# A second Strassen level for two of the seven products of the MLP gates, with the weight pass issued by GpSimd

## The chip, the cores and the metric

The kernel runs on one core of one Trainium2 chip. The metric is device time in microseconds (us), the median of several executions. One profiled execution stands beside it; all rows below come from that one.

## What is computed

A decoder layer on x of shape (2, 512, 1024), all in fp32. Only the parts around the change matter here:

```python
h  = res + mamba2(rmsnorm(res, ln1_w), ...)          # ends in y @ w_out.T
h2 = rmsnorm(h, ln2_w)
x  = x + h + silu(h2 @ gate_w.T) * (h2 @ up_w.T) @ down_w.T      # the MLP, inner width 3584
x  = x + cross_attention(layernorm(x), ctx)          # quantised to 8-bit codes
def _binary_diff_weight(w, base):
    d = w - base
    return base + mean(abs(d)) * sign(d)
x  = x + ffn(layernorm(x), W1, W3, W2)               # same form as the MLP, W_j = _binary_diff_weight(w_j, mean_w_j)
```

The three FFN weights need a mean over all of |w - base| before the first of them can be used. The kernel therefore makes one pass over w1, w3 and w2 (the weight pass) while the MLP runs.

## The kernel before, in words

**Stages.** In order of time: mamba up to its gated output; the out product (y @ w_out.T, 28 tiles on TensorE, L565) with the second RMS norm and its transposes (`finish`, L576 to L584), here called the turn; the MLP gates (about 470 to 1159 us); the MLP down product (to about 1490 us), with the cross-attention woven in; the FFN gates; the FFN down product.

**Tiling of the gates.** 3584 inner columns are cut into 14 groups of 256. A group has a gate weight and an up weight of 1024 x 256, and each is multiplied with the activations of 2 x 512 tokens as a 2x2 block product by Strassen's scheme in Winograd's form: seven block products instead of eight, each of them 4 matmuls of 128x128 by 128x512. Gate and up together take 56 such matmuls per group. The class `BlockProduct` (L227 to L272) holds one such product; `gates` (L649 on) runs the groups. `weight_blocks` makes the sums of weight blocks on VectorE (DVE), `act_blocks` (once) those of the activations. The seven products are added up on DVE from four PSUM banks. ScalarE (ACT) applies silu, DVE multiplies gate by up (L687), `hidden_blocks` and `down_blocks` (both through the helper at L192 and L195) make the sums of blocks that the down product needs, and these are stored in DRAM.

**The FFN gates** use another function, `gates2` (L766 on). There gate and up are stacked and a second level of Winograd's scheme is put on some of the seven products: products 1 and 2 (together) and 6 and 7 (together) become seven smaller products of four 128x256 matmuls each (`second_level`, L721 to L747), and the others (c: products 5 and 3, d: product 4) stay as 128x512 matmuls at L813.

**The weight pass.** `abs_sums` (L1008 on) is called once per MLP group. For each of the three weights it loads w and base on SyncE's queue (SP), 1 MB each (L177), subtracts on GpSimd (POOL, L1015), takes the sign into a bf16 tile on ACT (L1017), stores it from SP (L1018, 512 KB), and takes the absolute sum on ACT (L1019). All loads and stores of the MLP stand in one SP queue, in program order, and a waiting instruction holds up those behind it. For the first eight groups, ctx is turned to codes here too.

**What sets the order.** Each engine works through its own instructions in order. A scheduler lays out the streams from the order of the program; `tc.issue_after(x)` puts a piece no earlier than instruction x. In the FFN stage `in_turn` writes the order of TensorE (PE) out by hand. Pools give the number of buffers: one place for a gate weight and one for an up weight of the next group in `gates` (pool w, 2 places in all).

Of the kernel before, what the change touches and what calls it, by code (L numbers as in the profile page):

```python
# [37 lines left out]
def decoder(ctx, tc, a, out):  # L38
# [136 lines left out]
    def load_w(wp, tag, src, name, shape=(P, KC, GW)):  # L175
        wt = wp.tile(list(shape), F32, tag=tag, name=name)
        nc.sync.dma_start(wt, src)  # L177
        return wt
# [105 lines left out]
    def hidden_blocks(h):  # L284

        a11, a12, a22, a21, s2, s3, s4 = (h[:, i, :] for i in range(7))
        sub(s3, a11, a21)
        add(a21, a21, a22)
        sub(s2, a21, a11)
        sub(s4, a12, s2)  # L290

# [3 lines left out]
    with ExitStack() as m:  # L295
# [232 lines left out]
        scanned(1)  # L528

# [29 lines left out]

        def out_product(p, use):  # L560
            for t in range(TPB):
                ps = bank(count[0] % 4, f"op{p}_{t}")
                count[0] += 1
                for k in range(4):
                    nc.tensor.matmul(  # L565
                        ps, A[p][:, k, t * P : t * P + P], B[p][:, k, :], start=(k == 0), stop=(k == 3)
                    )
                use(t, ps)
# [4 lines left out]

        def finish(t):
            b = t // TPB
            if t % TPB == 0:  # L576
                h2T.append(actp.tile([P, KC, L], F32, tag="act", name=f"h2T{b}"))
            h2 = rows.tile([P, D], F32, tag="ra", name=f"h2_{t}")
            rr = rms_scale(f"rms2_{t}", xr[t], h2)
            nc.scalar.activation(h2, xr[t], AF.Identity, scale=rr)  # L580
            to_feature_major("h2T", trans, h2, h2T[b], t, ln2, split=False)
            x = rows.tile([P, D], F32, tag="ra", name=f"xa{t}")
            nc.sync.dma_start(x, a["x"][t * P : (t + 1) * P, :])
            nc.gpsimd.tensor_tensor(xr[t], xr[t], x, ALU.add)  # L584
# [37 lines left out]
        out_product(3, use3)  # L622
        out_product(4, use4)
        scan.close()

    POOLS = dict(t8=1, w=2, w1=2, raw=2, ap=1, sp=2, hp=1, tmp=7, p1=2, o12=2, o67=1, px=2, s23=1, s4=2, y12=1, y67=1, b4=2, t4=1)

    def open_pools(g, name, names):  # L630

        pl = {x: g.enter_context(tiles_waited(name=f"{name}{x}", bufs=POOLS[x])) for x in names}
        return pl

    def first_products(name, act, pl, gw, uw):

        first = {1: act[0][:, :4, :], 2: act[0][:, 4:, :]}
        both = []
        for odd, (x, w) in enumerate((("g", gw), ("u", uw))):
            p = BlockProduct((odd, 2 + odd, 4 + odd, 6 + odd), pl, f"{name}{x}0", {1: w[:, :4, :P], 2: w[:, 4:, :P]}, first)  # L640
            p.weight = w
            both.append(p)
        for p in both:
            p.begin()
        for p in both:
            p.c11()
        return both

    def gates(name, act, acts, g, pl, weights, side, begun):  # L649


        dram = [
            [tc.dram_tile([P, 7, 512], F32, name=f"{name}{x}d{i}") for i in range(NG)] for x in ("h", "w")
        ]
        with g:
            B = act_blocks(name, act, [pl["ap"].tile([P, 4, L], F32, tag=f"t{i}", name=f"{name}t{i}") for i in (2, 3, 4)])
            for i in range(NG):
                gw, uw, t8 = weights(i)
                if i in begun:
                    gate, up = begun[i]  # L660
                    for p in (gate, up):
                        p.A, p.B = weight_blocks(pl["sp"], p.name, p.weight), B
                else:
                    gate, up = (
                        BlockProduct(
                            (odd, 2 + odd, 4 + odd, 6 + odd), pl, f"{name}{x}{i}",
                            weight_blocks(pl["sp"], f"{name}{x}{i}", w), B,
                        )
                        for odd, (x, w) in enumerate((("g", gw), ("u", uw)))
                    )  # L670
                gc = gate.others() if i in begun else gate.whole()
                last = i == NG - 1

                def down_weights(t8, after):
                    with tc.issue_after(after):
                        down_blocks(t8[:, :4, :], t8[:, 4:, :])
                    nc.sync.dma_start(dram[1][i], t8[:, 1:, :])

                down_weights(t8, gate.last)
                sg = [gate.t("s")] + list(gc[1:])  # L680
                for o, c in zip(sg, gc):
                    nc.scalar.activation(o, c, AF.Silu)
                side(i, pl["raw"])
                uc = up.others() if i in begun else up.whole()
                h = pl["hp"].tile([P, 7, L], F32, tag="h", name=f"{name}h{i}")
                for slot, s_, u_ in zip((0, 3, 1, 2), sg, uc):
                    nc.vector.tensor_tensor(h[:, slot, :], s_, u_, ALU.mult)  # L687
                if last:
                    nc.sync.dma_start(dram[0][i][:, :3, :], h[:, :3, :])
                hidden_blocks(h)  # L690
                if last:
                    nc.sync.dma_start(dram[0][i][:, 3:, :], h[:, 3:, :])
                else:
                    nc.sync.dma_start(dram[0][i], h)
        acts.close()
        return dram
# [52 lines left out]
    def first_two(name, act, pl, i, gw, uw, banks):  # L749

        O = pl["o12"].tile([P, 2, 2, L], F32, tag="o", name=f"{name}o12_{i}")
        ps = []

        def step(p, x, w):
            if not p:
                ps.append(bank(banks[x], f"{name}a{x}_{i}"))
            for k in range(4):
                nc.tensor.matmul(  # L758
                    ps[x], w[:, 4 * p + k, :P], act[0][:, 4 * p + k, :],
                    start=not p and k == 0, stop=k == 3, skip_group_check=p > 0,  # L760
                )
            nc.scalar.copy(O[:, p, x, :], ps[x])  # L762

        return O, [lambda p=p, x=x, w=w: step(p, x, w) for p in range(2) for x, w in enumerate((gw, uw))]

    def gates2(name, act, acts, g, pl, weights, down_weight, begun, places):  # L766
# [4 lines left out]
        with g:  # L771
# [3 lines left out]
            ex = [x.rearrange("p a (b c d) -> p a b c d", b=2, c=2) for x in places]  # L775
            B67 = second_level_right(t23, ex[0][:, 0], ex[0][:, 1], ex[1][:, 0])
# [26 lines left out]
            for i in range(NG):  # L803
# [15 lines left out]
                if i in begun:  # L819
                    O12 = begun[i]  # L820
                else:
# [21 lines left out]
                if not last:  # L843
                    with tc.issue_after(turn):
                        if i + 1 not in begun:
                            A12 = outer_left(i + 1, *coming[0])
                        A, A67 = left(i + 1, *coming[0])
                if i == 0:
                    b = act[0].rearrange("p (q k) l -> p q k l", q=2)
                    B12 = second_level_right(b, ex[1][:, 1], ex[2][:, 0], ex[2][:, 1])  # L850
                if i + 2 < NG:
                    coming.append(weights(i + 2, stored))
                if not last:
                    w2.append(down_weight(i + 1, stored))
                t = pl["t4"].tile([P, 4, 512], F32, tag="t", name=f"{name}w{i}t")
                b = w2.pop(0)
                with tc.issue_after(turn):
                    down_blocks(b, t)
                nc.sync.dma_start(dram[1][i][:, :3, :], b[:, 1:, :])
                nc.sync.dma_start(dram[1][i][:, 3:, :], t)  # L860
# [132 lines left out]

    g = ExitStack()
    pl = open_pools(g, "m", ("t8", "w", "raw", "ap", "sp", "hp", "tmp", "p1"))
    cx = g.enter_context(tiles_waited(name="cx", bufs=1))
    sgp = g.enter_context(tiles_waited(name="sgp", bufs=2))

    def mlp_weights(i):
        gw = load_w(pl["w"], "w", a["gate_w"][i], f"gate{i}")  # L1000
        uw = load_w(pl["w"], "w", a["up_w"][i], f"up{i}")
        t8 = pl["t8"].tile([P, 8, 512], F32, tag="t8", name=f"down{i}")
        nc.sync.dma_start(t8[:, :4, :], a["down_w"][i])
        return gw, uw, t8
# [3 lines left out]
    def abs_sums(i, wp):  # L1008

        for j, (n, base) in enumerate(FFN):  # L1010
            w, b = (
                flat(load_w(wp, tag, a[x][i], f"s{x}{i}", (P, 4, 512) if n == "w2" else (P, KC, GW)))
                for tag, x in (("raw", n), ("base", base))
            )
            nc.gpsimd.tensor_tensor(w, w, b, ALU.subtract)  # L1015
            sg = sgp.tile([P, KC * GW], BF16, tag="sign", name=f"sg{n}{i}")
            nc.scalar.activation(sg, w, AF.Sign)  # L1017
            nc.sync.dma_start(signs[j][i], sg)  # L1018
            nc.scalar.activation(w, w, AF.Abs, accum_out=sums[:, j, i : i + 1])  # L1019
        if i < KC:  # L1020
            ctx_codes(i // 4, i % 4)

    loaded = [mlp_weights(0)]
    begun = first_products("m", h2T, pl, *loaded[0][:2])
    dram = gates("m", h2T, acts, g, pl, lambda i: loaded.pop() if loaded else mlp_weights(i), abs_sums, {0: begun})


# [276 lines left out]
```

## Time and profile before

| what | us |
|---|---|
| median of 3 executions (2448.77 to 2453.83) | 2449.19 |
| the profiled execution's own time | 2447.95 |
| its span, first to last instruction | 2446.1 |
| TensorE busy in the span | 2394.3 |
| granted TensorE clock, mean | 0.996 |
| the turn, 430 to 474 | 44.0 |
| MLP gates until the first down product (L911) | 474.0 to 1158.9 |
| most of the FFN gates | 1585 to 2143 |

How to read it: times are of one core. An engine's row gives busy time, number and mean duration of its instructions, and after the last bar its idle time ahead of them with what ended it ("<-"). fp32 matmuls appear as two records each, so a 128x512 matmul is two records of 0.429 us. PEclk is the share of full speed at which the chip let TensorE run. "DMA share" is the mean busy share of 16 DMA engines. In the timeline, a number in brackets is the idle time ahead of an instruction.

### The profile page before, as it was taken

To read this page: it belongs to the slowest core of one execution; us is meant where nothing else is said; L and a number is where in the kernel's file an instruction comes from. 1 tells how busy PE (TensorE), PEld (TensorE's weight loads), DVE (VectorE), ACT (ScalarE), POOL (GpSimd) and SP (SyncE) were. 2 spreads that over 40 slices of the span, in tenths; PEclk is the share of its full clock that TensorE was granted. 3 is DMA by queue.
4 is the path that set the end of the run, shared out by engine and by line. 5 is a ranking of instruction groups with operands and counts; after the bars stand their busy time and mean duration, and the time that the engine had idled before them with its cause. 6 is when DMAs were issued, how large, how long until landed. Compare 5 with 4: busy or idle time off the path is not lost.

```text
span 2446.1 us, 21791 instructions
## 1 busy us (share of the span) xinstructions
PE 2394.3 (98%) x8108; PEld 1485.6 (61%) x8116; DVE 1462.6 (60%) x2175; ACT 584.0 (24%) x704; POOL 314.6 (13%) x166
## 2 busy tenths in 40 slices
PE   7999999799999999999999999999999999999999
PEld 5445444444444444444888775567667667688888
DVE  4656676544544565444555656686675776665554
ACT  3222142443333433230000234332132221100000
POOL 1002020533323323220000010000000000000000
PEclk9999999999999999999999999999999999999999
DMA  3010032687888878875865480577667577686652
GB/s 139 35 52 18 18 121 100 236 325 297 345 313 336 342 314 339 312 297 180 250 186 166 123 264 35 154 202 198 190 181 203 166 197 207 221 259 193 201 168 65
DMA packets 177802, 486.00 MB, mean 199 GB/s; under 512 B 20768, under 2 KB 125216, under 8 KB 145696
## 3 DMA queue, kind: packets, MB, share of 16 engines
q1 hardware_dynamic: 171072, 436.37, 49.7%
q0 software_dynamic: 6624, 48.24, 9.6%
q8 instruction: 64, 1.05, 0.2%
q14 instruction: 42, 0.34, 0.0%
HBM read 345.07 MB, written 137.36 MB: 197 GB/s over the span
## 4 chain that ended last, share of the span: by engine, by line
PE 80%; DMA 7%; DVE 4%; POOL 4%; ACT 2%; issue 2%; SPq 1%; POOLq 0%; DVEq 0%; ACTq 0%
DMA smean_w<-in_mean_w 5%; POOL sw L1015 3%; PE op L565 3%; ACT sgw L1017 1%; DMA up<-in_up_w 1%; PE xa L1113 1%; DVE down L195 1%; PE dps L349 1%; PE fa L758 1%; PE y L485 1%; PE f0c L813 1%; PE f11c L813 1%; PE f10c L813 1%; PE f7c L813 1%; PE f4c L813 1%
## 5 line engine op out<-in xcount | busy, mean ns | idle before, releaser
L1015 POOL TENSOR_TENSOR sw<-sw,smean_w 128x2048 f32<-128x2048 f32 x42 | 196.6, 4681 | 405.5 <-DMA smean_w<-in_mean_w 401.3
L1017 ACT ACTIVATE sgw<-sw 128x2048 bf16<-128x2048 f32 x42 | 80.2, 1909 | 335.9 <-POOL sw L1015 335.9
L1195 POOL DMA_DIRECT2D fw<-in_mean_w x42 | 36.2, 861 | 527.6 <-ACT fw L1194 475.0
L1194 ACT ACTIVATE fw<-fsign,coeff 128x2048 f32<-128x2048 bf16 x38 | 76.1, 2004 | 93.6 <-DMA fsign<-sign 20.7
L1019 ACT ACTIVATE sw<-sw 128x2048 f32<-128x2048 f32 x42 | 80.2, 1909 | 0.9
L195 DVE TENSOR_TENSOR down<-down 128x512 f32<-128x512 f32 x56 | 77.7, 1408 | 0.7
L865 ACT ACTIVATE fo<-fo 128x512 f32<-128x512 f32 x56 | 35.0, 627 | 118.0 <-DVE fo L192 117.9
L511 POOL TENSOR_TENSOR mz<-mz,ys 128x512 f32<-128x512 f32 x16 | 20.7, 1293 | 309.2 <-DVE ys L508 277.1
L565 PE MATMUL op<-wout,mz 128*128 128x512 f32 x128 | 56.6, 592 | 0.0
L565 PEld LDWEIGHTS op<-wout,mz 128*128 128x128 f32 x128 | 23.9, 190 | 27.7 <-issue 27.5
L91 POOL TENSOR_TENSOR q_r<-q_e,mhalf 128x1 f32<-128x1 f32 x8 | 6.5, 806 | 260.9 <-DVE q_e L87 260.3
L867 DVE TENSOR_TENSOR fh<-fo 128x512 f32<-128x512 f32 x56 | 36.1, 682 | 1.5
L758 PE MATMUL fa<-x3T,fw 128*128 128x512 f32 x64 | 30.1, 624 | 2.1 <-ACT fo L762 2.1
L118 PE MATMUL h1T<-ident,h 128*128 128x128 f32 x64 | 15.2, 384 | 16.3 <-ACT h L340 10.4
L195 DVE TENSOR_TENSOR fh<-fh 128x512 f32<-128x512 f32 x42 | 29.0, 689 | 1.0
L195 DVE TENSOR_TENSOR mh<-mh 128x512 f32<-128x512 f32 x42 | 28.8, 686 | 0.5
L192 DVE TENSOR_TENSOR hid<-hid,op 128x512 f32<-128x512 f32 x24 | 15.9, 683 | 21.3 <-PE op L565 21.3
L1113 PE MATMUL xa<-c,c1T 128*128 128x512 bf16 x122 | 28.1, 379 | 0.3
L349 PEld LDWEIGHTS dps<-wdt,h1T 128*128 128x128 f32 x128 | 23.7, 272 | 2.4 <-issue 1.8
L161 ACT ACTIVATE cc<-ctx,back 128x2048 bf16<-128x2048 f32 x8 | 16.0, 1998 | 29.1 <-DVE ctx L160 29.1
L758 PEld LDWEIGHTS fa<-x3T,fw 128*128 128x128 f32 x64 | 12.4, 199 | 17.0 <-issue 14.0
L118 PEld LDWEIGHTS h1T<-ident,h 128*128 128x128 f32 x64 | 12.1, 223 | 16.8 <-ACT h L340 10.4
(2077 smaller groups left out, 5549.5 us busy)
## 6 DMA issues: line engine op xcount, KB each, us to landing
sw<-in_w SPq DMA_DIRECT2D x42, 1024.0 KB, 7.7
smean_w<-in_mean_w SPq DMA_DIRECT2D x42, 1024.0 KB, 9.2
fw<-in_mean_w POOLq DMA_DIRECT2D x42, 1024.0 KB, 13.6
mwd<-down SPq DMA_DIRECT2D x14, 1792.0 KB, 7.2
mhd<-mh SPq DMA_DIRECT2D x13, 1792.0 KB, 6.9
fhd<-fh SPq DMA_DIRECT2D x13, 1792.0 KB, 8.1
sign<-sgw SPq DMA_DIRECT2D x42, 512.0 KB, 3.0
fsign<-sign SPq DMA_DIRECT2D x38, 512.0 KB, 8.9
```

Source lines behind the costliest of these rows:

```text
L195: nc.vector.tensor_tensor(out_, x, y, ALU.subtract)
L349: nc.tensor.matmul(dps[:, t, :], h1T[t // TPB][:, k, c : c + P], wdt[:, k, :], start=(k == 0), stop=(k == KC - 1))
L565: nc.tensor.matmul(ps, A[p][:, k, t * P : t * P + P], B[p][:, k, :], start=(k == 0), stop=(k == 3))
L758: nc.tensor.matmul(ps[x], w[:, 4 * p + k, :P], act[0][:, 4 * p + k, :], start=not p and k == 0, stop=k == 3, skip_group_check=p > 0,)
L813: nc.tensor.matmul(into[x][j], A[j][p][:, k, :], B[p][:, k, :], start=not onto and k == 0, stop=k == 3, skip_group_check=onto,)
L867: nc.vector.tensor_tensor(h[:, slot, :], o[:, 0], o[:, 1], ALU.mult)
L1015: nc.gpsimd.tensor_tensor(w, w, b, ALU.subtract)
L1017: nc.scalar.activation(sg, w, AF.Sign)
L1019: nc.scalar.activation(w, w, AF.Abs, accum_out=sums[:, j, i : i + 1])
L1113: nc.tensor.matmul(ps, self.c1T[:, k, c : c + P], self.c2[k // 4][:, k % 4, hs], start=(k == 0), stop=(k == KC - 1))
L1194: nc.scalar.activation(dst, src, AF.Identity, scale=coeff[:, j : j + 1])
L1195: nc.gpsimd.dma_start(dst, a[base][i].rearrange("p a b -> p (a b)"), accum_op=ALU.add)
```

## The change

1. **MLP gates.** The old `gates` and its `BlockProduct` use are gone for this stage. `gates2` becomes `gates` and serves both stages. With `two=True` it does what it did for the FFN. With `two=False` (the MLP) products 6 and 7 go by the second level, while products 1 and 2 are plain (`first_two`, 16 matmuls of 128x512 per group), as are 3, 4 and 5 (24 of them).
2. **Residual rows.** The eight residual tiles (four pairs of 1 MB) are stored to DRAM ahead of the MLP gates (`spilled`) and their SBUF places hold what the second level needs; `reloaded` brings them back behind the gates, from GpSimd's queue. The FFN stage uses the same two helpers, so its reload moves from SP to GpSimd.
3. **Weights.** gate and up have two places each (pools w and w1, by parity of the group), on the right side of SBUF, and groups 0 and 1 are loaded before the last two out products. The loads of group i+2 are issued behind product d of group i.
4. **Weight pass.** Its loads and sign stores are issued by GpSimd and stand with the subtractions in one written order: store of sign n-1, load of n+1, subtraction of n. The load of the next group's w1 also waits for the DVE instruction `turn` of the group (L808). The sign is written over the base buffer, so a base buffer is loaded again only after the store of its sign has landed.
5. **The turn.** `finish` is split: `turned` does the transposes. The order of TensorE is written out: out tile, then the transposes of the tile two places earlier, and the first products of MLP group 0 behind the last tiles.
6. The places of the down product's operands are permuted.

The diff, cut to its core (`gates2` is taken over as `gates` with the changes shown; `first_two` and `in_turn` have only moved up):

```diff
+    def gate_up(pl, i, after=None):
+        with tc.issue_after(after) if after else nullcontext():
+            return [load_w(pl[("w", "w1")[i % 2]], "w", a[x][i], f"{x}{i}") for x in ("gate_w", "up_w")]
...
         def finish(t):
...
             nc.scalar.activation(h2, xr[t], AF.Identity, scale=rr)
-            to_feature_major("h2T", trans, h2, h2T[b], t, ln2, split=False)
+
+        def turned(t):
+            to_feature_major("h2T", trans, h2s.pop(t), h2T[t // TPB], t, ln2, split=False)
             x = rows.tile([P, D], F32, tag="ra", name=f"xa{t}")
             nc.sync.dma_start(x, a["x"][t * P : (t + 1) * P, :])
             nc.gpsimd.tensor_tensor(xr[t], xr[t], x, ALU.add)
...
-        out_product(3, use3)
-        out_product(4, use4)
-        scan.close()
+        mlp_weights = [gate_up(mpl, i) for i in (0, 1)]
+        begun_m, first_m = first_two("m", h2T, mpl, 0, *mlp_weights[0], (4, 5))
+        parts = [lambda t=t: out_tile(3, t, use3) for t in range(TPB)]
+        parts += [lambda t=t: out_tile(4, t, use4) for t in range(TPB)]
+        parts += first_m
+        for n, part in enumerate(parts):
+            in_turn(part)
+            if 2 <= n < 2 + NT:
+                in_turn(lambda: turned(n - 2))
...
                 if i in begun:
                     O12 = begun[i]
+                elif not two:
+                    O12, steps = first_two(name, act, pl, i, *coming[0], X)
+                    for step in steps:
+                        step()
                 else:
...
-                        if i + 1 not in begun:
+                        if two and i + 1 not in begun:
                             A12 = outer_left(i + 1, *coming[0])
                         A, A67 = left(i + 1, *coming[0])
...
+                side(i, turn)
                 for j in range(2):
                     add(O67[:, 0, j], O67[:, 0, j], c[j])
...
+    def spilled(name, after=None):
+        xd = tc.dram_tile([P, NT // 2, 2 * D], F32, name=f"{name}xd")
+        places = []
+        for j in range(NT // 2):
+            with tc.issue_after(after) if after else nullcontext():
+                nc.sync.dma_start(xd[:, j, :], flat(pairs[j]))
+            places.append(flat(xpool.tile([P, 2, D], F32, tag=f"x{2 * j}", name=f"{name}pl{j}")))
+        return xd, places
...
+    def load_diff(n_, after=None):
...
+            on_pool(lambda: nc.gpsimd.dma_start(tl, a[x][i].rearrange("p a b -> p (a b)")))
+            if after:
+                tc.add_manual_dep(
+                    pool_last[0], after.name,
+                    mybir.DependencyInfo(mybir.DependencyClass.Sync, mybir.DependencyReason.DATA), reason="pace",
+                )
...
+    def abs_sums(i, after):
         for j in range(3):
+            n_ = 3 * i + j
+            if not n_:
+                load_diff(0)
+            if unstored:
+                store_signs()
+            if n_ + 1 < len(diffs):
+                load_diff(n_ + 1, after if j == 2 else None)
+            w, b = raw.pop(n_)
+            on_pool(lambda: nc.gpsimd.tensor_tensor(w, w, b, ALU.subtract))
+            sg = b.bitcast(BF16)[:, : KC * GW]
             nc.scalar.activation(sg, w, AF.Sign)
+            unstored.append((i, j, sg))
             nc.scalar.activation(w, w, AF.Abs, accum_out=sums[:, j, i : i + 1])
...
-    down("m", dram, 512, (0, 1, 7, 3, 6, 5, 2, 8, 4, 9, 10, 11), ready, work)
+    down("m", dram, 512, (0, 1, 2, 6, 3, 4, 7, 5, 8, 9, 10, 11), ready, work)
```

In steady groups of the changed kernel (the fourth on) ACT's stream has the sign of w1 of a group directly ahead of the copy of that group's first product out of PSUM (L329), and TensorE's second step on that bank waits for the copy. VectorE's sums for the second level of group i+1 (`left`) stand between the instruction `turn` of group i and its hidden blocks.

## The prediction

> **What bounds the kernel now.** I read the page's busy row and its chain first.
>
> ```profile
> PE 2394.3 (98%) x8108; PEld 1485.6 (61%) x8116; DVE 1462.6 (60%) x2175; ACT 584.0 (24%) x704; POOL 314.6 (13%) x166
> PE 80%; DMA 7%; DVE 4%; POOL 4%; ACT 2%; issue 2%; SPq 1%; POOLq 0%; DVEq 0%; ACTq 0%
> ```
>
> TensorE works for 98% of the span and carries 80% of the chain. The other shares of the chain run through the weight pass while TensorE works too. So a change pays if it takes matmuls away or closes one of TensorE's few gaps, and costs if it opens a new one. Next I cut the touched stages out by windows (columns: us, then busy us of PE, weight loads, DVE, ACT, POOL, granted clock, DMA share, GB/s), and asked for TensorE's waits in the gates.
>
> ```profile
> 430.00:474.00 44.00, 31.46 (x115) 17.51 (x114) 24.27 (x38) 26.58 (x28) 23.98 (x15) 0.92 0.56 204
> 474.00:1148.00 674.00, 666.80 (x1543) 294.12 (x1542) 340.61 (x423) 217.90 (x215) 197.21 (x43) 0.99 0.80 311
> 1585.00:2143.00 558.00, 557.94 (x1980) 373.70 (x1979) 393.52 (x588) 126.31 (x134) 29.17 (x34) 1.00 0.69 196
> ```
> ```profile
> PE mg11b L238 <- DVE mg11u L192: 4.1, 1, 4.1
> PE mg5b L238 <- DVE mg5u L192: 2.6, 1, 2.6
> PE mg9b L238 <- DVE mg9u L192: 0.5, 1, 0.5
> ```
>
> The turn leaves TensorE idle for 12.5 us of 44; its timeline gives four gaps, 4.63, 2.68 and 2.99 behind the scaling of h (L580) and 2.24 behind the first gate weight. The MLP gates leave 7.2 idle. The FFN gates, which already use the second level, leave none: with DVE 71% busy the scheme can run at TensorE's pace.
>
> **The matmuls.** A 128x512 matmul is 0.858 us (two records of 0.429), a 128x256 one 0.432 (28 of them span 12.1). From 430.0 to the first down product at 1158.9 are 728.9 us: 14 groups of 56 x 0.858 = 672.7; the rest of the out tiles and transposes at full clock, 27.5; and 28.7 of idle time and half clock. A changed group has 40 x 0.858 + 28 x 0.432 = 46.4 instead of 48.05, so 14 groups take 649.6. If nothing waited, the stretch would be 27.5 + 649.6 = 677.1, that is 51.8 less: 23 from matmuls, 28.7 from gaps.
>
> **The turn.** Transposing two tiles later gives the norm of a tile about 7 us of other matmuls, against gaps of at most 4.63; the weights, now loaded before the last two out products, end the 2.24. I count the 12.5 as gone. What is late next: the residual rows. After the last x row is added on POOL (2.4 us, the shortest L584 spans) each 1 MB pair is stored (the FFN's stores landed after 10.1), and then four DVE sums of 1.25 make the second level's right side: about 20 with the x load ahead. Its cover is two first steps (6.9) and products 5 and 4 of group 0 (13.7), 20.6 together. So near balance; DVE also makes the activation sums then, 16 x 0.6. I charge 9 us for the first groups, half-clock time included (0 to 15).
>
> **The weight pass and its lock.** Each subtraction holds up DVE sums that read two SBUF tiles:
>
> ```profile
> 905.18 4.53 POOL L1015 TENSOR_TENSOR sw<-sw,smean_w 128x2048 f32<-128x2048 f32 x1 [12.57 <-DMA smean_w<-in_mean_w]
> 905.24 0.69 DVE L192 TENSOR_TENSOR mu8u<-mu8p,mu8b 128x512 f32<-128x512 f32 x1 [6.65 <-PE mu8b L238]
> 905.96 0.69 DVE L192 TENSOR_TENSOR mu8c<-mu8u,mu8c 128x512 f32<-128x512 f32 x1
> 906.68 0.69 DVE L192 TENSOR_TENSOR mu8u<-mu8u,mu8d 128x512 f32<-128x512 f32 x1
> 907.28 2.97 DVE L687 TENSOR_TENSOR mh<-mg8c,mu8c 128x512 f32<-128x512 f32 x1
> ```
>
> Three operations with a PSUM operand run at 0.69 beside it, the product of two SBUF tiles takes 2.97 and ends with the subtraction. DVE's own work is no bound: some 27 us a group, with three locks of 4.5 at most 41 of 46.4. But order matters. ACT takes the sign of w1 of a group ahead of copying that group's first product out of PSUM, and TensorE needs the copy for its second step. The sign waits for the subtraction, this for POOL's queue, and that reaches back to the `turn` of the group before. One lap, from `turn` (L808) to the next, in program order and with the rows of before (DVE 0.60 per sum back to back):
>
> - DVE: three sums 1.8, the subtraction of w2 4.5 with its start delayed by up to 0.5, eleven sums 6.6, ending with the first add of product 4: 13.0.
> - Then two ways meet. ACT and POOL: silu 0.65, absolute sum 2.1, 0.4 to POOL, two issues of 0.6 to 0.86, subtraction of w1 4.5 with up to 0.5: about 10.0. DVE: eight sums 4.8 and, if the subtraction locks the ninth, 4.5 and 0.4, then two more, 1.2, and a silu 0.65: 11.6. The lock meets the ninth sum or misses it by about 0.6 us, which the trace of before cannot settle.
> - Sign 1.95 and copy 0.7: 2.65.
> - TensorE: 8 x 0.858 + 28 x 0.432 = 19.0. Copy and two 1024-wide adds of 1.25: 3.5.
>
> Sum: 48.2 the short way, 49.8 the long, against 46.4 of TensorE work. So TensorE idles 1.8 or 3.4 in each of the eleven steady groups; in the first three the sign stands later.
>
> What is the gap worth? The Trainium skill ("TensorE: Matmul & The Clock Gate", section "Why this matters for your kernels") advises against idle gaps above about 3 us. By it, 1.8 costs only itself. Here a gap of 2.07 ahead of L758 at 1507 was followed by eight matmul records in 5.40 instead of 3.43, and 2.56 and 4.10 also by half clock, while 1.42 was not. So I let about a third of the 1.8 gaps cost another 1.7, and every 3.4 gap. Likeliest is 48.8: 11 x 2.4 = 26 us.
>
> **The moved queue.** Per group POOL issues nine DMAs, at 0.6 (L1192) to 0.86 (L1195) each, 5.4 to 7.7, beside 13.5 of subtraction: 21 of 46.4, no bound. SP loses what held its queue, so the gate and up weights come early; with two places each the gates' 7.2 us of gaps should go. The page shows what the loads of the pass need:
>
> ```profile
> smean_w<-in_mean_w SPq DMA_DIRECT2D x42, 1024.0 KB, 9.2
> fw<-in_mean_w POOLq DMA_DIRECT2D x42, 1024.0 KB, 13.6
> sign<-sgw SPq DMA_DIRECT2D x42, 512.0 KB, 3.0
> ```
>
> The load of the next w1 waits for `turn`; behind it on POOL stand its base, the subtraction of w2, the sign store and the loads of w3. Its own subtraction comes 18 us later (13.0 and 5.4), so 9.2 or even 13.6 fits. The base load waits for the sign store to land, 3.0, with about a microsecond to spare. The skill's formula for a GpSimd-issued DMA ("DMA: Bandwidth & Descriptors", section "Anatomy of one DMA — SWDGE (gpsimd) path", 2.0 us plus bytes at 436 GB/s) gives 4.4 for 1 MB, which would leave 13 of slack; the rows under load leave 4 to 9. I take the rows and charge nothing; if landing took 20, each lap would grow by 2 or more. Spill and reload add 8 MB, about 19 us of DMA at the 430 GB/s of the fullest short windows, against 0.2 x 674 = 135 idle: nothing. The reload is behind the last second level, and the FFN's same reload cost no gap: 0, to 5 at the edge. The permuted places: 0, within 1 us either way.
>
> **Sum.** 677.1 + 26 + 9 = 712, against 728.9: 17 less. From the profiled 2447.95 (1.85 outside the span) this is 2431.4; the median of before lies 1.2 higher, so 2433.
>
> **The rivals.**
>
> *Half clock in each lap (slower).* The subtraction of w1 catches the ninth sum, the gap is 3.4 and each also costs 1.7: a lap of 51.5. Then 677.1 + 11 x 5.1 + 9 = 742, 13 more: 2462. For it: the 0.6 us, and that the longer lap leaves the phase to repeat. Against: short issues, or an absolute sum that starts late, move the subtraction past that sum. It decides from a lap of about 50.5, where 11 x 4.1 + 9 eats the whole 51.8.
>
> *No loop.* The pass runs ahead so that the sign is never late: laps of 46.4 to 47.5. With 5 to 9 at the start that is 2402 to 2418. For it: FFN gates without a gap. Against: the load waits for `turn` in each group by construction.
>
> *The change doesn't close the turn, or the long way without half clock.* 12 us stay at the turn, or laps are 49.8 to 50.4: 2444 to 2453.
>
> **Chances.** Forecast (2422 to 2441) 0.37; no loop 0.13; unchanged 0.16; half clock 0.27; slower for another reason (late loads, a start above 15) 0.07. A measurement of this kernel tells 0.2% from no change, 4.9 us. Faster 0.50, same 0.16, slower 0.34. The range runs from 2404, the middle of the no-loop case's lower part, to 2464, past the half-clock value.
>
> **What would show it.** The turn: no gap above 1 us behind L580. Groups: 46.4 of matmuls each. The loop: once per group from the fourth on, TensorE waiting 1.5 to 3.5 us for the copy at L329, that copy standing behind the sign (L1057) and this behind the subtraction (L1055); laps of 48 to 50 between `turn` instructions. Half clock: the eight records after the gap in over 5 us instead of 3.43. Wrong would be: POOL waiting for loads, TensorE waiting for DVE sums (L195) instead of L329, or a stall above 15 us in groups 0 to 2.

## The result, and the profile after

The changed kernel takes 2540.8 us (median of 4, 2539.72 to 2544.36) against 2451.51 for the kernel before: a ratio of 1.0367, with a 95% interval of 1.0348 to 1.0386. The profiled execution took 2544.36, its span 2542.6, which is 96.5 more than before. The forecast was 2433. So nearly 110 us separate the forecast from the result.

The same two rows of the page, after:

```profile
PE 2405.9 (95%) x8452; PEld 1566.3 (62%) x8452; DVE 1575.0 (62%) x2277; ACT 615.1 (24%) x760; POOL 395.7 (16%) x300
PE 66%; DMA 9%; POOL 8%; DVE 8%; issue 5%; ACT 4%; SPq 0%; POOLq 0%; DVEq 0%; ACTq 0%
```

TensorE's busy time rose by 11.6 us although it has 23 us less to do: the granted clock was 0.979 over the run, where it had been 0.996. Its share of the chain fell from 80% to 66%. The stages (same columns as before; the gates now last until 1243, so their window is longer):

```profile
430.00:474.00 44.00, 39.85 (x138) 21.45 (x137) 28.02 (x45) 18.09 (x24) 18.95 (x17) 0.96 0.52 189
474.00:1232.00 758.00, 666.69 (x1856) 369.72 (x1855) 448.90 (x514) 270.09 (x279) 280.63 (x171) 0.94 0.74 283
1675.00:2230.00 555.00, 554.93 (x1986) 374.77 (x1985) 395.37 (x594) 126.26 (x134) 31.35 (x38) 1.00 0.68 194
```

The turn is better, the FFN gates are as they were, and the MLP gates have 91 us of idle time where they had 7, at a mean clock of 0.94. TensorE's waits, of the whole run, with the idle us, how often, and the longest:

```profile
PE ma L325 <- ACT mo L329: 18.9, 13, 3.4
...
PE mn0b L715 <- DVE mpl L192: 10.2, 1, 10.2
PE mo1e L888 <- DVE m1b L195: 9.5, 1, 9.5
PE mn2c L715 <- DVE mpl L192: 9.5, 1, 9.5
...
PE mn6b L715 <- DVE mpl L192: 5.3, 1, 5.3
...
PE mn8b L715 <- DVE mpl L192: 4.9, 1, 4.9
```

A wait on the second step of the small product b (mnXb) comes back in every group from the fourth on, in most at 4 to 6 us. The forecast had only the wait on the copy (L329). From one `turn` (L808) to the next it is 55.4 us, the mean from group 5 to group 12; the forecast was 48.8 and TensorE's own work is 46.4.

Here is the end of one such lap in the chain of waits (start, duration, what). "DMA sign" is the store of the sign of w1 until it has landed; the whole chain of this lap runs from the end of the turn at 842.24 to the end of the next at 897.24.

```profile
859.31 5.62 POOL sw L1055
864.94 0.02 issue
864.96 1.92 ACT smean_w L1057
866.88 0.40 issue
867.28 9.62 DMA sign<-smean_w
876.90 0.02 issue
...
878.10 4.54 POOL sw L1055
882.63 0.02 issue
882.66 1.91 ACT smean_w L1057
884.57 0.48 ACT mpl L722
885.05 0.02 issue
885.07 0.70 DVE mpl L192
```

GpSimd waits for the landing ahead of the next base load, and the subtraction of w3 stands behind that load in its stream. ACT has the sign of w3 ahead of copying the first small product (L722), so DVE's first sum and TensorE stand behind a 512 KB store. GpSimd's waits show that this is no single case; from 480 to 1200 us they are

```profile
POOL smean_w L1034 <- DMA sign<-smean_w: 105.4, 17, 9.4
```

and from 700 to 1160 alone 71.4 us in nine waits, about one per lap. TensorE shows the price in the lap above:

```profile
879.55 1.89 PE L715 MATMUL mn7d<-mpl,mu7s 128*128 128x256 f32 x8
885.81 3.78 PE L715 MATMUL mn7b<-mpl,mpl 128*128 128x256 f32 x8 [4.38 <-DVE mpl L192]
889.39 2.81 PE L715 MATMUL mn7a<-mt,mg7s 128*128 128x256 f32 x8
```

The gap is 4.38. Behind it the granted clock was 0.50 until 889.6 and 0.69 until 892.2, which adds 1.9 and 0.9: 7.2 of the lap. This is what was issued in those ten microseconds (KB each, us to landing):

```profile
mhd<-mh SPq DMA_DIRECT2D x1, 1792.0 KB, 11.1
sw<-in_w POOLq DMA_DIRECT2D x1, 1024.0 KB, 11.1
sign<-smean_w POOLq DMA_DIRECT2D x1, 512.0 KB, 9.6
```

The hidden blocks (1.8 MB) were issued 1.1 us behind the store and the next w2 2.4 us behind it; a down weight of 1 MB, issued 2.7 us ahead of it, was still under way. While the store was out, the DMA share was 1.01 and the engines moved 391 GB/s. The same lap's other two stores, from the same queue, met less traffic: the sign of w2, issued at 850.91, landed after 4.8 us, and that of w3, issued at 884.97, after 2.9. In the eight laps from 740 to 1165 us w1's took 9.5 to 11.6, w2's 4.8 to 5.0 and w3's 2.9 to 3.2. So GpSimd's queue as such did not make the store slow. That the traffic of the moment did is what fits; no run takes this traffic away.

### The profile page after: what moved, and what is told of

It is laid out like the page before. It is cut to its first block, busy times and chain, and to the rows that moved or that the text cites. A ratio compares the mean times of both kernels' runs of the same rounds, so it can differ in the third digit from the quotient of the medians.

```text
span 2542.6 us, 22703 instructions
## 1 busy us (share of the span) xinstructions
PE 2405.9 (95%) x8452; PEld 1566.3 (62%) x8452; DVE 1575.0 (62%) x2277; ACT 615.1 (24%) x760; POOL 395.7 (16%) x300
## 4 chain that ended last, share of the span: by engine, by line
PE 66%; DMA 9%; POOL 8%; DVE 8%; issue 5%; ACT 4%; SPq 0%; POOLq 0%; DVEq 0%; ACTq 0%
POOL sw L1055 6%; DMA sign<-smean_w 5%; PE op L606 3%; ACT smean_w L1057 2%; DMA ctx<-in_ctx 2%; DVE mpl L192 1%; DMA xa<-in_x 1%; PE fa L325 1%; PE dps L390 1%; POOL smean_w L1034 1%; DVE mpl L808 1%; POOL hid L632 1%; PE y L526 1%; PE xa L1157 1%; PE f0c L785 1%
## 5 line engine op out<-in xcount | busy, mean ns | idle before, releaser
L1057 ACT ACTIVATE smean_w<-sw 128x2048 bf16<-128x2048 f32 x42 | 80.2, 1909 | 202.9 <-POOL sw L1055 202.9
L325 PE MATMUL ma<-h2T,gate_w 128*128 128x512 f32 x224 | 105.7, 616 | 18.9 <-ACT mo L329 18.9
L325 PE MATMUL ma<-h2T,up_w 128*128 128x512 f32 x224 | 100.9, 592 | 0.0
L1237 ACT ACTIVATE fw<-fpl,coeff 128x2048 f32<-128x2048 bf16 x38 | 76.0, 2003 | 95.3 <-DMA fpl<-sign 23.4
L325 PEld LDWEIGHTS ma<-h2T,gate_w 128*128 128x128 f32 x224 | 42.8, 197 | 77.2 <-issue 47.9
L325 PEld LDWEIGHTS ma<-h2T,up_w 128*128 128x128 f32 x224 | 42.5, 190 | 53.4 <-issue 53.4
L844 DVE TENSOR_TENSOR mh<-mpl 128x512 f32<-128x512 f32 x28 | 51.1, 1827 | 2.7 <-ACT mpl L842 1.4
L329 ACT COPY mo<-ma 128x512 f32<-128x512 f32 x56 | 32.0, 578 | 49.4 <-PE ma L325 45.0
L1043 POOL DMA_DIRECT2D sign<-smean_w x42 | 24.5, 583 | 110.5 <-ACT smean_w L1057 110.5
L195 DVE TENSOR_TENSOR down<-down 128x512 f32<-128x512 f32 x56 | 38.2, 683 | 0.0
## 6 DMA issues: line engine op xcount, KB each, us to landing
fw<-in_mean_w POOLq DMA_DIRECT2D x42, 1024.0 KB, 14.1
```

Of the source, the lines that this page charges most:

```text
L195: nc.vector.tensor_tensor(out_, x, y, ALU.subtract)
L325: nc.tensor.matmul(ps[x], w[:, 4 * p + k, :P], act[0][:, 4 * p + k, :], start=not p and k == 0, stop=k == 3, skip_group_check=p > 0,)
L844: nc.vector.tensor_tensor(h[:, slot, :], o[:, 0], o[:, 1], ALU.mult)
L1237: nc.scalar.activation(dst, src, AF.Identity, scale=coeff[:, j : j + 1])
```

## The experiments

Three theories. L: the lap is closed through the landing of w1's sign. P: it is closed through the pace, the wait of the next w1 load for the turn (GpSimd idles about 12 us there in each group; the chain above starts with it). D: DMA traffic as a whole sets it. The laps below are means from the turn of group 5 to that of group 12. The runs up to own_twice were executed once each, on two chips where the kernel before took 2459.1 and 2452.7, so there the laps weigh more than the times.

**The sign in a place of its own** (own_sign). px keeps one buffer of two, in another place, and the sign gets the place that the two had; nothing else moves.

```diff
-    pl["px"] = Room(*(ex[3][:, k : k + 2 * Q].rearrange("p (a b) -> p a b", a=2) for k in (0, 2 * Q)))
+    own_sign = ex[3].bitcast(BF16)
+    pl["px"] = Room(places[3][:, 3 * 4 * P :].rearrange("p (a b) -> p a b", a=2))
...
-            sg = b.bitcast(BF16)[:, : KC * GW]
+            sg = own_sign
```

> Theory L (landing): each steady lap of 55.0 us is closed through the landing of w1's sign store (9.6 us): the sign lies over the base buffer, so GpSimd waits for that landing before it can load the next base, and the subtraction of w3, its sign and the copy of the first small product stand behind. Here the sign has a place of its own, all else is as in the changed kernel. L: laps of 47 to 49.5, the waits of TensorE on the second mnXb step fall from about 5 to under 1 per lap, profiled time 2463 (2450 to 2475). Rival D (DMA): the landing is slow because the 16 engines are full in that stretch; with this wait gone GpSimd waits for its loads instead (L1055 on DMA), laps stay at 52 or more, time 2520 or more. Rival P (pace): the wait of the next w1 load for the turn, 12 us of GpSimd per lap, closes the lap; then this run gains under 20 us: 2520 to 2540.

2481.1, on a chip where the kernel before took 2459.1. The lap is 48.0. TensorE's waits from 700 to 1160 us are now:

```profile
PE ma L325 <- ACT mo L329: 12.6, 10, 3.3
PE mn8b L715 <- DVE mpl L192: 1.4, 1, 1.4
```

The waits on b are gone but for one, that on the copy stayed. The chain of waits now runs the way that the prediction had laid out, three laps in a row from 726.8 to 870.5, with the sign of w1 (L1058) between the subtraction and TensorE's second step:

```profile
841.02 5.62 POOL sw L1056
846.66 1.91 ACT mpl L1058
849.10 7.13 PE ma L325 x16
```

The lap is what L said; the time is 18 above its value and 6 above its range: gaps at the start of the stage and at its end (below) remained that the expectation had set too low, and the kernel before took 8 more on this chip. P had 2520 or more and falls here as the sole cause: the pace still stands.

**The signs behind the copies** (copy_first). The landing wait stays, but TensorE no longer stands behind it. `copied` holds the two copies; the lines that fill it are left out.

```diff
...
+            with tc.issue_after(copied[("m", i)]) if j == 0 else tc.issue_after(copied["p1"]) if j == 1 else nullcontext():
-            nc.scalar.activation(sg, w, AF.Sign)
+                nc.scalar.activation(sg, w, AF.Sign)
```

> Only ACT's order is changed: the sign of w1 behind the copy of the group's first gate product, the sign of w3 behind the copy of the first small product; the store still lands before the base load. L: TensorE no longer hangs on the landing, laps of 46.4 to 50 (then GpSimd's own lap), the idle at L329 and mnXb both under 1 per lap, time 2455 to 2480. D: laps of 52 or more, 2520 or more. P: the pace is as before, but nothing of TensorE waits behind it: no statement on ACT's order, at most 20 less, 2520 to 2540.

2479.3 on the same chip, and a lap of 47.1, both as L said; from 710 to 1150 us TensorE waits 4.4 us in all, at the copies. The landing can stay if nothing that TensorE needs is queued behind it.

**No pace** (no_pace).

```diff
-                load_diff(n_ + 1, after if j == 2 else None)
+                load_diff(n_ + 1)
```

> Only the wait of the next w1 load for the turn is taken out; sign over base and the landing wait stay. P: laps of 47 to 49, time 2450 to 2475. L: GpSimd starts each w2 subtraction earlier, by 3 to 8 us, but the landing waits stay in front of each subtraction: a lap of 49 to 53, time 2480 to 2520. D: 2520 or more.

2522.6, a lap of 52.5. The lap lies in L's range and the time a little above it; P's range is far off, and D's 2520 or more would fit as well. It is not a clean test. Without the pace the scheduler moved the signs to other places among ACT's copies, and the waits at L329 grew:

```profile
PE ma L325 <- ACT mo L329: 46.7, 11, 6.9
```

What the pace alone costs is read from a later pair.

**Both** (own_copy: own_sign and copy_first together).

> A sign place of its own and both signs behind the copies. L: laps of 46.4 to 47.5, that is TensorE's own work; left are the stalls of the first three groups and the one at the first down product, time 2445 (2432 to 2458). D: 2520 or more, with GpSimd waiting for loads. P: 2500 or more, since the pace stands.

2469.4; the lap is 46.46, and from 710 to 1160 us TensorE has no wait at all. So the second level does run at TensorE's own pace beside the whole weight pass, its locks included. The time is 24 above L's value and 11 above its range: gaps of 36 us in the first four groups and the turn, and 14 at the first down product, remained.

**Each sign stored twice** (twice, on the changed kernel; own_twice, on own_copy).

```diff
...
+        on_pool(lambda: nc.gpsimd.dma_start(again[j][i], sg))
         on_pool(lambda: nc.gpsimd.dma_start(signs[j][i], sg))
```

> The changed kernel, with each sign stored twice (a second 512 KB to a place that nobody reads, issued ahead of the real one); the sign still lies over the base buffer, so GpSimd's next base load waits for both. Theory L: one landing per lap is on the path; doubling it adds 0.6 of issue and 1.2 (at full rate) to 5 (at the rate it got, 9.6 for 512 KB beside others): laps of 57 to 60, time 2565 to 2605. Rival D (all DMA traffic together sets the lap, 14 MB of it): 1.5 MB more per lap adds 1.5/14 of 55, some 6 per lap, here and where the sign has its own place.

> The kernel with a sign place of its own and both signs behind the copies (own_copy, 2469), with each sign stored twice in the same way. L: nobody waits for the landing but the next sign, which comes some 14 us later, so laps stay at 46.4 to 47.5: 2465 to 2485. D: 6 per lap as with the shared buffer: 2530 or more.

twice took 2523.6, which is *less* than the changed kernel and far below the 2565 to 2605 of L. Its streams say why: with the extra instructions the scheduler put both signs behind the copies, as in copy_first, so copy_first is its base (chosen after the result, for this reason). Against that it is 44 us more, a lap of 50.7 against 47.1. Its chain of waits shows the two landings that come to bear in each lap:

```profile
847.27 7.69 DMA sign<-smean_w
...
863.67 11.58 DMA sign<-smean_w
```

own_twice took 2467.0, within L's range, with own_copy's lap of 46.46. (own_copy took 2469.4, on the chip where the kernel before was 6 slower.) The same added bytes cost 3.6 us per lap where the next load waits for the landing, and nothing where it doesn't. D, which asked for 6 in both, falls: the bytes had room.

**The start.** Before, six of the eight ctx steps ran ahead of the gates (ACT's parts of them from 372 to 469 us) and the last two at 773 and 821. In the changed kernel all eight run in the first four groups, from 494 to 676. ACT's stream in group 2, and DVE's step behind it:

```profile
598.89 0.59 ACT L722 COPY mpl<-mn2a 128x512 f32<-128x512 f32 x1
608.72 2.09 ACT L159 ACTIVATE ctx<-ctx,x_zp,inv_x 128x2048 f32<-128x2048 f32 x1 [9.25 <-DMA ctx<-in_ctx]
610.72 1.89 ACT L1057 ACTIVATE smean_w<-sw 128x2048 bf16<-128x2048 f32 x1
610.85 1.23 DVE L160 TENSOR_SCALAR ctx<-ctx 128x2048 f32<-128x2048 f32 x1 [10.65 <-ACT ctx L159]
```

ACT waits 9.25 us for ctx, and DVE's ctx step (L160), behind that one in turn, stands ahead of sums that TensorE needs: this is the 9.5 at mn2c. ctx_later is own_copy with these steps moved to later groups, one in each; ctx_nopace also drops the pace.

```diff
...
-        if i < KC:
-            ctx_codes(i // 4, i % 4)
+        k = i - 4
+        if 1 <= k <= KC:
+            with tc.issue_after(copied["p1"]):
+                list(begun_ctx.pop())
+        if 0 <= k < KC:
+            with tc.issue_after(after):
+                begun_ctx.append(ctx_codes(k // 4, k % 4))
+                next(begun_ctx[0])
```

> As own_copy (own sign place, signs behind the copies), and the codes of ctx, which stood bunched in the first four groups, are worked one per group from the sixth group on. Theory L, second part: with the laps at 46.4, what is left of the loss is 36 us of gaps (and the half clock behind them) in groups 0 to 3, where ACT's ctx steps wait for their 1 MB load ahead of copies that TensorE needs, and 14 at the first down product. L: gaps in groups 0 to 3 fall to 10 to 20, time about 25 below own_copy's 2469: 2445 (2436 to 2455), that is below the kernel before by 5 to 20. Rival S (start): the gaps are those of the spilled residual rows and the activation sums, not of ctx; then the gain is under 8: 2461 or more.

> As ctx_later, and the next w1 load no longer waits for the turn. The 14 us at the first down product come from its operand loads: their places are those of the weight pass, which in the last group ends some 10 us ahead of the gates' end. L: without the pace the pass ends 5 to 10 earlier and the gap at mo1e shrinks by as much: 2437 (2428 to 2448). Rival P (the pace keeps the subtraction off the steps that TensorE waits for): laps rise above 47, time 2455 or more.

ctx_later took 2436.1 (median of 13) against 2453.8 on its chip: a ratio of 0.9929 (0.9918 to 0.994). own_copy was 10 above the kernel before on its chip and this is 18 below: some 28 gained, where L had 25 and S under 8, so S falls. Run once more beside the next kernel (ctx_later_2) it gave 0.9931 (0.9916 to 0.9946). The gaps in the turn and groups 0 to 3 fell from 36 to 12, against 10 to 20 expected. ctx_nopace took 2435.3, a ratio of 0.9925 (0.9904 to 0.9947), a lap of 46.8 against 47.6: with the signs out of the way the two times differ by less than 1 us, which is within the noise. The gap at mo1e stayed (12.8 against 14.1), so the second half of that expectation failed.

> The same kernel as ctx_later, beside early_end on one chip: 2436 as before, gap at mo1e of 14.

**The end** (early_end). ctx_later, with four weights in each of groups 9 to 11 and none in the last, and the ctx steps two groups earlier.

```diff
+    counts = [3] * 9 + [4] * 3 + [3, 0]
...
-        for j in range(3):
-            n_ = 3 * i + j
+        for j in range(counts[i]):
+            n_ = sum(counts[:i]) + j
```

> As ctx_later, but the weight pass works four weights in each of groups 9 to 11 and none in the last group, so it ends a group earlier (ctx codes in groups 3 to 10). What is left of the loss after ctx_later is a gap of 14.1 us at the first down product (mo1e), laid to its operand loads, whose places are the weight pass's buffers. Theory: the gap falls under 4, the time to 2422 (2414 to 2430). Rival: the operands are late because their own last stores (weights and hidden blocks of group 13) are late; then the gap stays above 10 and the time at 2433 or more. Four weights in a lap could also make TensorE wait again, 2 to 5 per lap.

2434.4 against 2454.3, a ratio of 0.9932 (0.991 to 0.9954): the same as ctx_later, and outside the 2414 to 2430 that was expected. The gap at mo1e is gone altogether. Its operand loads were indeed waiting for the weight pass's buffers: in ctx_later_2 SP's queue holds them for ACT's last sums over these buffers,

```profile
SPq L880 <- ACT sw L1064: 21.2, 2, 10.9
```

and in early_end these waits are over by 1090 us, 54 ahead of the first down product. But the expected 14 did not come out, since the fuller laps opened two gaps at the copies, each with half clock behind it:

```profile
1002.87 6.22 PE L327 MATMUL ma<-h2T,gate_w 128*128 128x512 f32 x8 [5.39 <-ACT mo L331]
1055.46 5.40 PE L327 MATMUL ma<-h2T,gate_w 128*128 128x512 f32 x8 [3.35 <-ACT mo L331]
```

Eight records take 3.6 at full clock, so these two give back 8.7 and some 4.

## Why the prediction was wrong

From 430 us to the first down product it took 813.2 us; the forecast for that stretch was 712, with 677.1 if nothing waited. The 136 above that floor lie so: 52 until the turn of group 3 (forecast 9), 86 in the ten laps from there (forecast some 26), less 2 at the end. The other 12 of the 96.5 lie behind it, at the first down product (forecast 0 to 5).

- **The matmuls: right.** 46.46 per lap in own_copy against 46.4. (The forecast's last sum gives 2431.1, not 2431.4; nothing hangs on it.)
- **The turn: mostly right.** The 12.5 of idle time were counted as gone; one gap of 4.15, ahead of the last transposes, is left of the four, and the lower clock behind it adds 1.5. Why the last tile was late was not looked into.
- **The lap: right in form, wrong in one link.** The short way, 48.2, is what own_sign runs: 48.0, and not by luck. In its lap from 822.71 the copy behind w1's sign ends 26.3 after the turn (forecast 25.7), TensorE's part takes 19.3 (19.0) and the last sums 2.1 (3.5). The step that failed is "The base load waits for the sign store to land, 3.0, with about a microsecond to spare" and the "charge nothing" that followed. The landing took 9.6 in the lap shown and 9.5 to 11.6 in eight laps, so the wait that was put at nothing ends last and closes the lap. The two ways can be set side by side from the end of w1's sign. One is the landing, a load's issue 1.15, the subtraction 4.5, the sign 1.9, copy and sum 1.2, with 0.4 ahead. The other is the copy, two first steps of 6.9 in all and four small ones of 6.9. That is 9.2 plus the landing against 14.2: 2.0 to spare at 3.0, 4.6 late at 9.6. The trace has 4.38. The price of half clock makes it 7.2; with 46.4 of work and 1.0 for the wait at the copy that is 54.6, and this lap took 55.0.
- **Why the 3.0 was the wrong figure.** It is a median over 42 stores, and the trace of before already held their spread:

```profile
DMA to landing us min/median/max: 2.6/3.0/9.1
```

With 9.1 in place of 3.0 the step does not hold. In the changed kernel the median from 640 to 1140 us is 4.9, which by the sum above would be almost harmless (14.1 against 14.2); the one that decides is w1's, which is issued about a microsecond ahead of the hidden blocks. I kept both ends for the loads (9.2 and 13.6), not for the store.

- **The start: a size that was not costed.** The prediction charged 9 (0 to 15) for the spilled rows and the activation sums, and had no term for ctx, whose steps moved into the first groups. The spill's wait did show (3.96 ahead of a DVE sum), but most of the 52 is ctx: taking it out of the first groups brought the turn of group 3 from 677 (in own_copy, as in the changed kernel) to 642, 35 us. Why the scheduler put the steps there was not looked into. "A start above 15" stood among the rivals, at 0.07 together with late loads.
- **The end: a place, not a time.** The permuted places were given 0; what counted was that the pass now holds its buffers nearly to the end of the gates: its last sign was stored at 1222.7 of 1243, where before it had been 1078.6 of 1159.
- **The lock: right that it is no bound.** The rival "half clock in each lap" named the right consequence, but by another way: not the ninth sum, the landing.

That ctx_later comes within 4 us of the forecast is no confirmation of it: its stretch to the first down product is 703.9, where the forecast had 712, and 14.1 are lost behind it, where the forecast had 0 to 5.

What the 12 us at the first down product are beyond the 9.5 gap and the lower clock behind it was not taken apart. The pace on the changed kernel alone was not measured, as its removal moved ACT's order too.

## What to carry to other kernels

A buffer whose content is being stored is free only when the store has landed; price that landing in the traffic of that very moment, not by the median of the page, and look who stands behind the waiting instruction on its engine, and behind that on the next. When a side job shares in-order engines with the main path, put its steps behind those that the bound engine needs: the order of ACT's stream alone was worth some 60 us here (2540.8 to 2479.3, one execution, on another chip). A scheduler may change that order when an unrelated instruction is added, so compare streams before two times.

## What the runs showed of the hardware

Whether a gap of TensorE costs half clock did not go by its length alone. A gap of 2.16 us ahead of L326 (own_copy, at 705) was followed by eight records in 5.40 at a granted clock of 0.68, and one of 2.51 (own_copy, at 687) by 5.40 too. A gap of 3.43 ahead of L325 (twice, at 865) was followed by 3.70 at a granted clock of 1.00, while 3.32 at 915 was followed by 5.25 at 0.70. All gaps of 1.0 to 1.7 in the gates of these runs were followed by full clock. The Trainium skill ("TensorE: Matmul & The Clock Gate", section "What's actually happening") speaks of a free-running window of 3413 ns that does not start with the work. That would fit, with the gap's place in the window deciding; no run here shows the window itself.

Landing times: a store of 512 KB took 3.0 us in the median of before (2.6 to 9.1) and 4.9 after. Within one lap of the changed kernel it took 2.9, 4.8 and 9.6, from the same queue; the last had the DMA share at 1.01, with three larger transfers under way.
